# A planner's costs and ranks replaced: shorter VectorE and ScalarE costs, a weight-load lag ahead of products, and new ranks

## The chip, the cores and the metric

The kernel runs on one core of a Trainium2 chip. The metric is the device time in microseconds (us) of one execution. Engines are named as in the profile: PE is TensorE (PEld its weight loads), DVE is VectorE, ACT is ScalarE, POOL is GpSimd, and SP is SyncE, which here only issues DMAs.

## What is computed

A batch of 128 graphs with 128 nodes and 256 features goes through four layers. Each starts with a layer norm and a ReLU and adds its result to the residual x. Three layers are graph attention, one is a gated graph network of three GRU steps. Cut to what matters:

```python
def gat(h, adj, W, a):                      # layers 0, 1, 2
    Wh = einsum('bnf,fo->bno', h, W)
    e = (Wh @ a1)[:, :, None] + (Wh @ a2)[:, None, :]
    e = where(e > 0, e, 0.2 * e)
    att = softmax(where(adj > 0, e, -9e15), axis=-1)
    return elu(einsum('bij,bjo->bio', att, Wh))

def ggnn(x, adj, weight, w_ih, w_hh, b_ih, b_hh):   # layer 3
    A = (adj != 0)
    h = x
    for i in range(3):
        m = einsum('bnd,de->bne', h, weight[i])
        aggr = einsum('bst,bsd->btd', A, m)
        h = gru_cell(aggr, h, w_ih, w_hh, b_ih, b_hh)
    return h

for layer in (gat0, gat1, gat2, ggnn):
    x = x + layer(relu(layernorm(x)), adj)
```

All data is float32.

## The kernel before

**Groups and stages.** The 128 graphs are cut into 33 groups: one of two graphs, 31 of four, and one of two. Group g runs through three attention layers (`attention`, stages 0 to 2), a norm (stage 3, in `gat`), and three recurrent steps (`gru`, `step`). All groups share the engines; x has buffers for six groups in flight.

**An attention layer**, with the lines of the program before: VectorE's statistics (`stats`, L519), GpSimd's scaling and power for the inverse deviation (L525, L528), ScalarE's normalisation (xn, L602), VectorE's score sums (scr, L610, two for each graph). In the first two groups (`far` false) TensorE turns the scores into rows (L638) and the weights (L695), and VectorE scales them (at, L702). In later groups the rows go through DRAM (er), and the weights are transposed in blocks by VectorE (L552) and brought into place by two DMAs (d_at at L559, at at L563). Between lie ScalarE's slope (L649), VectorE's mask and maximum (L660, L662), ScalarE's exponential (L666) and scaling (L679). Then TensorE gathers neighbours (ahp, L723), ScalarE copies the sum (ah, L730), TensorE projects (hp, L742), and ScalarE and VectorE apply the ELU and add to x (L756, L758, L760).

**A recurrent step** is written as Strassen-like block products: TensorE aggregates in two halves (agp, L991), ScalarE copies each half (ag, L999), VectorE forms differences (t13, t24, L929, L923), TensorE makes the gate products (a, e, b, L965; nn, nnb, L952; ni, L1047), ScalarE and VectorE move partial sums between banks (L1015, L1099, L1106), ScalarE applies the tanh (L1035, L1052), VectorE mixes the new state. In the middle groups the new state is transposed by VectorE and sent through DRAM (`turned_state`, L580 and L584). The first two and the last two groups turn it on TensorE instead (hnp, L852).

**Setup.** Before the first recurrent step the weights are made: sums for the attention vectors (L325, L330), transposes of w_hh, w_ih and the layer weights (L410), products of w_ih with them (wcp, wcn, L466), ScalarE's copies out of the banks, and GpSimd's sums and differences of weight blocks (`combinations`, L388, L396).

**What sets the order.** No engine instruction is issued in the order of the program text. Every operation is handed to a planner (`Plan.add`) with its engine, an assumed cost in us, a rank, and the tiles that it reads and writes; a DMA (`Plan.load`) is an operation of SP with a cost of 0.45 and a landing time. `Plan.issue` then runs a list schedule: of the operations that are ready on an engine within `WINDOW` of the earliest, it takes the one of the lowest rank, and holds back those whose rank lies more than `AHEAD` (or, while the lowest rank left is up to `UNTIL`, `EARLY`) above the lowest rank still left. `lag` is what it adds between an operation and one that depends on it: per producing engine when another engine reads the result, nothing on the same engine. The list that comes out is issued as it stands; each engine then works through its own queue in that order on the chip, waiting on semaphores. The costs and ranks are thus used only to fix the order. They do not change what an instruction does.

Costs are given by the number of columns: `pe(c) = 0.006 + c/600`, `dve(c) = 0.145 + c/960`, `act(c) = 0.25 + c/1400`, `pool(c) = 0.35 + c/512`. Ranks come from tables: `SETUPS` for the setup, `ATT` for the stages of the first groups, `STARTS` for the recurrent steps of the first groups, and formulas (`stage`, `start`) for all later ones. Operations that empty a bank get the rank of their step less `URGENT`.

Of the kernel before, what the change touches and what calls it, by code (L numbers as in the profile page):

```python
# [14 lines left out]
P = 128  # L15
# [24 lines left out]
class Plan:  # L40
# [2 lines left out]

    LAG = {"PE": 0.26, "DVE": 0.2, "ACT": 0.2, "POOL": 0.15}
    WINDOW = 0.097
    AHEAD = 4.12
    EARLY = 5.00
    UNTIL = -1.46  # L50

    def __init__(self):
        self.ops, self.writers, self.readers, self.rings = [], {}, {}, {}
# [10 lines left out]
    def add(self, engine, cost, rank, fn, reads=(), writes=(), after=(), takes=()):  # L64


        reads = [k if isinstance(k, tuple) else (k, None) for k in reads]
        writes = [k if isinstance(k, tuple) else (k, None) for k in writes]
        vals = list(dict.fromkeys(v for v, _ in reads + writes))
        vals += [v for v in dict.fromkeys(takes) if v not in vals]  # L70
        op = Op(engine, cost, rank, fn, vals)
        for v in vals:
            v.ops.append(op)

        def others(book, key):
# [24 lines left out]
        for d in op.deps:  # L100
            d.users.append(op)
        self.ops.append(op)
        return op

    def lag(self, d, engine, data=True):
        if d.engine == "SP":
            return d.lands
        return 0.0 if d.engine == engine else self.LAG[d.engine] if data else 0.08

    def issue(self):  # L110
        waits_for = {op: len(op.deps) for op in self.ops}
# [77 lines left out]
def kernel(  # L189
# [25 lines left out]
    nc = tc.nc  # L215
# [25 lines left out]
    add, load = plan.add, plan.load  # L241
# [24 lines left out]
    def dve(cols):  # L266
        return 0.145 + cols / 960
# [12 lines left out]
    mhalf = const.tile([P, G], FT, name="mhalf")  # L280
    nc.vector.memset(mhalf, -0.5)

    SETUPS = [-4.77, -3.63, -3.63, -3.63, -3.63, -3.63, -3.63]
    setting = [0]

    def setup_rank():
# [18 lines left out]
    W, VA = [], []  # L305

    def attention_weights(l, w, a):
        rank = [-6.42, -7.21, -4.35][l]
        wt, va = const_val(f"w_{l}", [KD, D]), const_val(f"va_{l}", [2, D])
        first = [-11.17, -10.17, -7.80][l]  # L310
        load(256, first, lambda: nc.sync.dma_start(
            wt.t, w.rearrange("(k p) o -> p k o", p=P)), writes=[wt])
        ar = val(su, "ar", [2 * D], f"ar_{l}")
        load(2, first - 0.1, lambda: nc.sync.dma_start(
            ar.t[:1, :], a.rearrange("n o -> o n")), writes=[ar])

        ab = bank("gat", f"ab_{l}")
        add("PE", pe(T), rank, lambda: nc.tensor.matmul(
            ab.t, ones[:1, :], ar.t[:1, :], start=True, stop=True), reads=[ar], writes=[ab])
        wa = val(su, "wa", [2, KD], f"wa_{l}")  # L320
        vp = bank("gat", f"vp_{l}")

        def one(s, k):
            scr = val(su, "scr", [D], f"scr_{l}_{k}_{s}")
            add("DVE", dve(D) + 0.08, rank, lambda: nc.vector.scalar_tensor_tensor(  # L325
                scr.t, wt.t[:, k, :], 1.0, ab.t[:, s * D : (s + 1) * D], op0=OP.mult, op1=OP.mult,
                accum_out=wa.t[:, s, k : k + 1],
            ), reads=[wt, ab], writes=[scr, (wa, (s, k))])
            c = s * KD + k
            add("PE", 0.11, rank, lambda: nc.tensor.transpose(  # L330
                vp.t[:, c * P : (c + 1) * P], wa.t[:, s, k : k + 1].to_broadcast([P, P]), ident
            ), reads=[(wa, (s, k))], writes=[(vp, c)])

        for s in range(2):
            for k in range(KD):
                one(s, k)
        add("ACT", act(T), rank, lambda: nc.scalar.copy(
            va.t.rearrange("p s d -> p (s d)"), vp.t), reads=[vp], writes=[va])
        W.append(wt)
        VA.append(va)  # L340
# [195 lines left out]
                nm.t, st.t[:, :, 1], -1.0, None, op0=OP.mult), reads=[st], writes=[nm])  # L536
        return nm, rs

    def exchanged(srcs, cut, dst, name, n, rank):

        kd = len(srcs)
        f = kd * n * 32
        tr = val(gw, f"tr{kd}", [Q, kd * G * 32], f"tr_{name}", bufs=3 - kd)
        d = plan.val(
            dram, f"d{kd}_{n}", 2,
            lambda: dram.tile([Q, 32, Q, f], FT, tag=f"d{kd}_{n}", name=f"d_{name}"),
        )
# [20 lines left out]
    def turned_state(src, k, dst, name, n, rank):  # L570


        tr = val(gw, "trs", [G, P], f"tr_{name}", cut=n)
# [3 lines left out]
        add("DVE", dve(n * P), rank, lambda: nc.vector.transpose(  # L577
            tr.t.rearrange("p b j -> p (b j)"), src.t[:, k, : n * P]
        ), reads=[(src, k)], writes=[tr], takes=[d, dst])
        load(64 * n, rank, lambda: nc.sync.dma_start(d.t.rearrange("b p f -> p b f"), tr.t),  # L580
            reads=[tr], writes=[d])

        def back(j):
            load(16 * n, rank, lambda: nc.sync.dma_start(  # L584
                dst.t[j * 32 : (j + 1) * 32, : n * P].rearrange("c (m r) -> c m r", r=32),
                d.t[:, :, j * 32 : (j + 1) * 32].rearrange("b (q c) r -> c (b q) r", q=Q),
            ), reads=[d], writes=[(dst, j)])
# [240 lines left out]
    def gru(g, xt, am, hn0, h0):  # L828
# [39 lines left out]
        def flat(h):  # L868

            def part(k):  # L870
                add("DVE", 0.42, start(g, 0) - 1.0, lambda: nc.vector.tensor_copy(
                    cut(h.t[:, k, :TG]), first(k)), reads=[h0], writes=[(h, k)], after=[*after, *begun])

            for k in range(KD):
                part(k)

        def step(i, h):
# [202 lines left out]
            def mixed(c):  # L1080
# [50 lines left out]
        def end(h):  # L1131
# [40 lines left out]

    ATT = [
        [-8.90, -4.73, -3.23, -1.30],
        [-7.16, -4.64, -3.85, -2.65],
        [-3.70, -1.92, 1.59, 3.59],
        [-0.38, 1.67, 4.29, 4.81],
        [3.81, 5.72, 6.93, 8.03],
        [7.96, 10.27, 13.26, 12.41],
        [9.50, 11.75, 14.74, 15.00],  # L1180
        [12.46, 14.80, 17.00, 18.00],
        [15.66, 17.97, 20.00, 21.29],
        [18.50, 20.75, 23.00, 24.00],
    ]
    STARTS = [
        [1.68, 2.28, 4.42],
        [3.03, 4.63, 6.47],
        [5.97, 6.79, 10.50],
        [9.00, 11.18, 12.82],
        [12.28, 14.00, 16.00],  # L1190
        [14.67, 16.85, 19.17],
        [17.30, 19.87, 22.34],
        [21.00, 23.00, 25.06],
    ]
# [53 lines left out]
```

## Time and profile before

| | |
|---|---|
| median of three runs | 2569.77 us |
| lowest and highest run | 2566.48 and 2571.89 us |
| the profiled execution, its own time | 2566.74 us |
| its span, first to last instruction | 2565.0 us |
| DVE busy | 2105.9 us, 82% |
| ACT busy | 1768.5 us, 69% |
| POOL busy | 225.1 us, 9% |
| mean granted TensorE clock | 0.993 |

The page's list of engines is read as shares of the span; a busy TensorE means that some matmul is in flight, not that it works at its peak. The chain that ended last runs through TensorE for 95% of the span:

```profile
PE 95%; DVE 2%; ACT 2%; DMA 1%; issue 0%; SPq 0%; POOL 0%; ACTq 0%; DVEq 0%
```

The costliest groups of instructions show durations, which for VectorE and ScalarE are longer than the distance at which two of them can start one behind the other:

```profile
L610 DVE SCALAR_TENSOR_TENSOR scr<-xn,va 128x256 f32<-128x256 f32 x732 | 270.3, 418 | 36.1 <-ACT xn L602 35.8
L756 ACT ACTIVATE t<-hp 128x512 f32<-128x512 f32 x192 | 104.6, 595 | 201.3 <-PE hp L742 201.2
L758 DVE SCALAR_TENSOR_TENSOR x<-hp,x 128x512 f32<-128x512 f32 x192 | 124.0, 685 | 71.0 <-ACT t L756 70.9
```

After the bar stand the busy time in us, the mean duration in ns, and, after the second bar, the idle time of the engine ahead of these instructions with what ended it.

### The profile page before, as it was taken

The numbers are of one execution on the slowest core, as the hardware profiler recorded it, in microseconds if no ns is written. First come the engines' busy times: TensorE is split into PE (matmuls) and PEld (weight loads), VectorE is DVE, ScalarE is ACT, GpSimd is POOL, SyncE is SP. The second block draws the span as 40 slices with busy tenths as digits, with TensorE's granted clock in tenths as the row PEclk, the third lists the DMA queues.
The fourth block names the chain that finished last, engine by engine and source line by source line (L and its number), as shares of the span: only waits on it lengthen the run. The fifth ranks groups of instructions, "written<-read, shape, count | busy, mean of one in ns | idle before, by whom it ended". The sixth has DMA issues, their size and how long they took to land.

```text
span 2565.0 us, 39018 instructions
## 1 busy us (share of the span) xinstructions
PE 2527.7 (99%) x12549; PEld 2098.6 (82%) x12549; DVE 2105.9 (82%) x4955; ACT 1768.5 (69%) x4411; POOL 225.1 (9%) x328
## 2 busy tenths in 40 slices
PE   8799999999999999999999999999999999999998
PEld 5688888888888888888888888888888888888887
DVE  6778888888888888888888888888888888888765
ACT  6777676776766776766776666776666777666554
POOL 2210000000000000000000000000000000000000
PEclk8899999999999999999999999999999999999999
DMA  3113343343343333343334333333334443333320
GB/s 106 46 57 97 87 111 108 95 108 95 106 109 99 107 104 95 108 107 103 105 102 96 109 104 106 104 100 100 107 103 104 107 99 101 101 89 97 75 62 13
DMA packets 503123, 245.75 MB, mean 96 GB/s; under 512 B 280579, under 2 KB 472067, under 8 KB 502918
## 3 DMA queue, kind: packets, MB, share of 16 engines
q1 hardware_dynamic: 502918, 243.25, 35.3%
q8 instruction: 100, 1.64, 0.3%
q14 instruction: 105, 0.86, 0.1%
HBM read 139.28 MB, written 103.87 MB: 95 GB/s over the span
## 4 chain that ended last, share of the span: by engine, by line
PE 95%; DVE 2%; ACT 2%; DMA 1%; issue 0%; SPq 0%; POOL 0%; ACTq 0%; DVEq 0%
PE b L965 19%; PE hp L742 13%; PE e L965 13%; PE ni L1047 13%; PE a L965 13%; PE ahp L723 7%; PE agp L991 6%; PE nn L952 6%; PE nnb L952 5%; ACT em L666 0%; DVE scr L610 0%; ACT em L679 0%; PE hnp L852 0%; DMA at<-d_at 0%; ACT hn L791 0%
## 5 line engine op out<-in xcount | busy, mean ns | idle before, releaser
L742 PE MATMUL hp<-w,ah 128*128 128x256 f32 x1536 | 356.2, 384 | 0.5 <-ACT ah L730 0.5
L1047 PE MATMUL ni<-ag,wc_n 128*128 128x512 f32 (+1 forms) x792 | 352.9, 580 | 0.9 <-DVE ni L1041 0.9
L742 PEld LDWEIGHTS hp<-w,ah 128*128 128x128 f32 x1536 | 286.7, 191 | 61.9 <-ACT ah L730 13.1
L610 DVE SCALAR_TENSOR_TENSOR scr<-xn,va 128x256 f32<-128x256 f32 x732 | 270.3, 418 | 36.1 <-ACT xn L602 35.8
L1047 PEld LDWEIGHTS ni<-ag,wc_n 128*128 128x128 f32 x792 | 147.1, 190 | 125.2 <-issue 104.0
L756 ACT ACTIVATE t<-hp 128x512 f32<-128x512 f32 x192 | 104.6, 595 | 201.3 <-PE hp L742 201.2
L1052 ACT ACTIVATE wn<-ni,bi 128x512 f32<-128x512 f32 (+1 forms) x198 | 133.4, 674 | 157.5 <-PE ni L1047 114.5
L991 PEld LDWEIGHTS agp<-am,hn 128*128 128x128 f32 x1536 | 204.7, 191 | 42.7 <-issue 30.8
L991 PE MATMUL agp<-am,hn 128*128 128x128 f32 x1536 | 208.9, 275 | 3.6 <-ACT ag L999 3.0
L525 POOL TENSOR_SCALAR ve<-st 128x4 f32<-128x4 f32 (+1 forms) x132 | 28.4, 215 | 2087.8 <-DVE st L519 1735.5
L965 PE MATMUL a<-h,whh_rz 128*128 128x256 f32 (+1 forms) x792 | 208.8, 373 | 0.8 <-ACT z L1035 0.5
L723 PEld LDWEIGHTS ahp<-at,xn 128*128 128x128 f32 x1536 | 190.6, 196 | 23.0 <-issue 14.4
L602 ACT ACTIVATE xn<-x,nm,rs 128x256 f32<-128x256 f32 x366 | 201.1, 594 | 3.8 <-DVE nm L531 3.8
L965 PE MATMUL a<-ag,wc_rz 128*128 128x256 f32 (+1 forms) x792 | 199.1, 373 | 0.0
L723 PE MATMUL ahp<-at,xn 128*128 128x128 f32 x1536 | 192.5, 279 | 4.6 <-DMA at<-d_at 2.8
L758 DVE SCALAR_TENSOR_TENSOR x<-hp,x 128x512 f32<-128x512 f32 x192 | 124.0, 685 | 71.0 <-ACT t L756 70.9
L519 DVE BATCH_NORM_STATS2 st<-x 128x6 f32<-128x512 f32 x256 | 170.3, 690 | 2.6 <-DMA x<-in_x_dram 2.5
L649 ACT ACTIVATE em<-er,e 128x128 f32<-128x128 f32 x366 | 164.3, 523 | 2.4 <-DMA er<-de 2.3
L666 ACT ACTIVATE em<-em,nmx 128x128 f32<-128x128 f32 x384 | 149.4, 392 | 11.6 <-DVE nmx L662 11.4
L965 PEld LDWEIGHTS a<-h,whh_rz 128*128 128x128 f32 x792 | 140.9, 191 | 16.9 <-issue 0.7
L965 PEld LDWEIGHTS a<-ag,wc_rz 128*128 128x128 f32 x792 | 141.1, 191 | 15.2 <-issue 0.5
L528 POOL TENSOR_TENSOR rs<-ve,mhalf 128x4 f32<-128x4 f32 (+1 forms) x132 | 144.0, 1091 | 11.0
(158 smaller groups left out, 5541.3 us busy)
## 6 DMA issues: line engine op xcount, KB each, us to landing
d_hn<-tr_hn SPq DMA_DIRECT2D x116, 256.0 KB, 2.4
hn<-d_hn SPq DMA_DIRECT2D x464, 64.0 KB, 2.3
er<-de SPq DMA_DIRECT2D x90, 256.0 KB, 3.9
d_at<-tr_at SPq DMA_DIRECT2D x90, 256.0 KB, 2.2
at<-d_at SPq DMA_DIRECT2D x360, 64.0 KB, 2.0
x<-in_x_dram SPq DMA_DIRECT2D x31, 512.0 KB, 5.0
d_h<-tr_h SPq DMA_DIRECT2D x31, 512.0 KB, 2.7
h<-d_h SPq DMA_DIRECT2D x124, 128.0 KB, 2.7
```

What stands on the lines that cost most here:

```text
L519: add("DVE", dve(T), rank, lambda: nc.vector.bn_stats(st.t[:, b, :].rearrange("p b s -> p (b s)"), xt.t[:, b, :].rearrange("p b d -> p d b ...
L528: add("POOL", 1.04, rank, lambda: nc.gpsimd.tensor_tensor(rs.t, ve.t, mhalf[:, :n], op=OP.pow), reads=[ve], writes=[rs])
L602: add("ACT", 0.45, rank, lambda: nc.scalar.activation(xn.t[:, b, :], xt.t[:, b, :], AF.Relu, bias=nm.t[:, b : b + 1], scale=rs.t[:, b : b ...
L610: add("DVE", dve(D), rank, lambda: nc.vector.scalar_tensor_tensor(scr.t, xn.t[:, b, :], 1.0 if far else rs.t[:, b : b + 1], VA[l].t[:, s, ...
L649: add("ACT", 0.55 if far else 0.42, rank, lambda: nc.scalar.activation(em.t[:, b, :], e2_row(b), AF.Prelu, bias=e.t[:, 0, b : b + 1], alph ...
L666: add("ACT", 0.42, rank, lambda: nc.scalar.activation(em.t[:, b, :], em.t[:, b, :], AF.Exp, bias=nmx.t[:, b : b + 1], accum_out=sm.t[:, b ...
L723: add("PE", pe(P), rank, lambda: nc.tensor.matmul(summed(ps, b), xn.t[:, b, k * P : (k + 1) * P], turned_weights(b), start=True, stop=True ...
L742: add("PE", pe(D), rank, lambda: nc.tensor.matmul(hp.t[:, b * D : (b + 1) * D], ah.t[:, k, c * P : (c + 1) * P], W[l].t[:, k, :], start=(k ...
L952: op = add("PE", pe(H), at, lambda: nc.tensor.matmul(ps.t[:, o : o + H], WHH[1].t[:, blk, :], rhs(), start=starts, stop=True, skip_group_c ...
L965: nc.tensor.matmul(ps.t[:, gate * D : gate * D + H], w[0].t[:, blk, gate * P : (gate + 1) * P], rhs(), start=go, stop=w is not WHH, skip_g ...
L991: nc.tensor.matmul(ps.t[:, b * P : (b + 1) * P], s, am.t[:, b, :], start=True, stop=True)
L1047: add("PE", pe(TG), rank + 0.45 + 0.05 * c, lambda k=k: nc.tensor.matmul(ni[c].t[:, :TG], WC[i][1].t[:, k, c * P : (c + 1) * P], ag.t[:, k ...
```

## The change

The planner's assumptions and the ranks are replaced; no operation is added, removed or altered.

- **Costs.** VectorE operations over 0.3 us are planned 0.08 shorter (but at least 0.08), the others 0.02 shorter; ScalarE operations 0.10 shorter.
- **Lags.** A result of VectorE, ScalarE or GpSimd for another engine is planned 0.02, 0.04 and 0.05 later. A result that the same engine reads is now planned 0.10 (VectorE, ScalarE) or 0.05 (GpSimd) later, where it was 0. Whatever TensorE needs of an engine other than itself and SP gets 0.25 more (`TO_PE`), also where it only waits for a bank or buffer to come free.
- **Ranks.** New numbers in `SETUPS`, in the attention weights' ranks, in `ATT` (15 groups given by hand instead of 10) and `STARTS`, a new formula for later groups (`LATE`), new `AHEAD`, `EARLY`, `UNTIL` and `URGENT`.
- **Separate ranks.** In `exchanged` the VectorE transposes take a rank of their own (`later`), used for the final output; in `turned_state` the DMAs take `rank - 1.0` of the step, and the transpose keeps `quick`.

```diff
-    LAG = {"PE": 0.26, "DVE": 0.2, "ACT": 0.2, "POOL": 0.15}
-    WINDOW = 0.097
-    AHEAD = 4.12
-    EARLY = 5.00
-    UNTIL = -1.46
+    LAG = {"PE": 0.26, "DVE": 0.22, "ACT": 0.24, "POOL": 0.2}
+    SELF = {"DVE": 0.1, "ACT": 0.1, "POOL": 0.05}
+    TO_PE = 0.25
+    WINDOW = 0.09700
+    AHEAD = 3.80719
+    EARLY = 4.99516
+    UNTIL = 4.33848
...
+        if engine == "DVE":
+            cost = max(0.08, cost - 0.08) if cost > 0.3 else cost - 0.02
+        elif engine == "ACT":
+            cost -= 0.1
         op = Op(engine, cost, rank, fn, vals)
...
-        return 0.0 if d.engine == engine else self.LAG[d.engine] if data else 0.08
+        if d.engine == engine:
+            return self.SELF.get(engine, 0.0) if data else 0.0
+        return (self.LAG[d.engine] if data else 0.08) + (self.TO_PE if engine == "PE" else 0.0)
...
-    SETUPS = [-4.77, -3.63, -3.63, -3.63, -3.63, -3.63, -3.63]
+    SETUPS = [-6.84787, -3.92921, -3.63418, -3.63418, -3.49802, -3.63418, -4.69368]
...
-        rank = [-6.42, -7.21, -4.35][l]
+        rank = [-7.18052, -6.81219, -4.64144][l]
...
-        first = [-11.17, -10.17, -7.80][l]
+        first = [-11.17390, -10.51150, -3.60698][l]
...
-    def exchanged(srcs, cut, dst, name, n, rank):
+    def exchanged(srcs, cut, dst, name, n, rank, later=0.0):
...
-            add("DVE", dve(n * P), rank, lambda: nc.vector.transpose(
+            add("DVE", dve(n * P), rank + later, lambda: nc.vector.transpose(
...
-        load(64 * n, rank, lambda: nc.sync.dma_start(d.t.rearrange("b p f -> p b f"), tr.t),
+        load(64 * n, moved, lambda: nc.sync.dma_start(d.t.rearrange("b p f -> p b f"), tr.t),
...
-                    turned_state(hnew, c, ahead[c], f"hn_{g}_{i + 1}_{c}", n_g, quick)
+                    turned_state(hnew, c, ahead[c], f"hn_{g}_{i + 1}_{c}", n_g, quick, rank - 1.0)
...
-                    o, f"o_{g}", n_g, rank,
+                    o, f"o_{g}", n_g, rank, 1.0 - URGENT,
...
-    URGENT = 1.00
-    SPAN = 2.25
-    HEAD = 5.5
+    URGENT = 0.99051
...
-    LEAD = 8.5
+    LATE = [-7.38300, -5.94660, -3.05880, -2.41780]
...
-        [-8.90, -4.73, -3.23, -1.30],
-        [-7.16, -4.64, -3.85, -2.65],
-        [-3.70, -1.92, 1.59, 3.59],
+        [-10.03150, -5.73666, -4.29186, -3.57801],
+        [-6.37019, -5.24915, -3.99721, -2.27005],
+        [-3.69791, -1.82237, 1.40914, 4.51073],
...
-        [1.68, 2.28, 4.42],
-        [3.03, 4.63, 6.47],
+        [1.67988, 2.28262, 3.67109],
+        [2.73703, 4.08406, 6.35165],
...
-        return ATT[g][l] if g < len(ATT) else 3.0 * g - LEAD + (SPAN * l if l < 3 else HEAD)
+        return ATT[g][l] if g < len(ATT) else 3.0 * g + LATE[l]
...
-        return STARTS[g][i] if g < len(STARTS) else 3.0 * g + 2.0 * i
+        return STARTS[g][i] if g < len(STARTS) else 3.0 * g + [0.0, 2.00000, 4.00000][i]
```

More of the change, by code (lines that the diff above doesn't have):

```diff
@@ L568, in exchanged, with turned_state @@
             back(j)
-    def turned_state(src, k, dst, name, n, rank):
+    def turned_state(src, k, dst, name, n, rank, moved):
         tr = val(gw, "trs", [G, P], f"tr_{name}", cut=n)
@@ L579, in turned_state @@
         ), reads=[(src, k)], writes=[tr], takes=[d, dst])
-        load(64 * n, rank, lambda: nc.sync.dma_start(d.t.rearrange("b p f -> p b f"), tr.t),
+        load(64 * n, moved, lambda: nc.sync.dma_start(d.t.rearrange("b p f -> p b f"), tr.t),
             reads=[tr], writes=[d])
         def back(j):
-            load(16 * n, rank, lambda: nc.sync.dma_start(
+            load(16 * n, moved, lambda: nc.sync.dma_start(
                 dst.t[j * 32 : (j + 1) * 32, : n * P].rearrange("c (m r) -> c m r", r=32),
@@ L870, in part @@
             def part(k):
-                add("DVE", 0.42, start(g, 0) - 1.0, lambda: nc.vector.tensor_copy(
+                add("DVE", 0.42, start(g, 0) - URGENT, lambda: nc.vector.tensor_copy(
                     cut(h.t[:, k, :TG]), first(k)), reads=[h0], writes=[(h, k)], after=[*after, *begun])
@@ L1170 @@
     NNR = 0.25
-    LEAD = 8.5
+    LATE = [-7.38300, -5.94660, -3.05880, -2.41780]
     ATT = [
-        [-8.90, -4.73, -3.23, -1.30],
-        [-7.16, -4.64, -3.85, -2.65],
-        [-3.70, -1.92, 1.59, 3.59],
[L1177 to L1183, printed above, removed]
+        [-10.03150, -5.73666, -4.29186, -3.57801],
+        [-6.37019, -5.24915, -3.99721, -2.27005],
+        [-3.69791, -1.82237, 1.40914, 4.51073],
+        [-1.21335, 2.94736, 3.53217, 4.28927],
+        [3.27576, 4.87639, 7.15969, 9.03665],
+        [8.55092, 10.98350, 13.51910, 13.24740],
+        [10.20170, 12.51510, 13.94510, 15.66230],
+        [13.68410, 16.44050, 18.86210, 20.30620],
+        [15.59690, 17.95450, 18.50160, 23.00030],
+        [18.45420, 20.96390, 22.85330, 24.29900],
+        [22.61700, 24.05340, 26.94120, 27.58220],
+        [25.61700, 27.05340, 29.94120, 30.58220],
+        [28.61700, 30.05340, 32.94120, 33.58220],
+        [31.61700, 33.05340, 35.94120, 36.58220],
+        [34.61700, 36.05340, 38.94120, 39.58220],
     ]
     STARTS = [
-        [1.68, 2.28, 4.42],
-        [3.03, 4.63, 6.47],
[L1188 to L1193, printed above, removed]
+        [1.67988, 2.28262, 3.67109],
+        [2.73703, 4.08406, 6.35165],
+        [5.98936, 8.53152, 10.05390],
+        [9.67922, 12.11970, 12.62760],
+        [12.27650, 13.52560, 16.00000],
+        [15.60350, 16.50370, 19.23710],
+        [17.36150, 20.71520, 22.17790],
+        [21.77790, 23.54310, 24.41420],
     ]
     def stage(g, l):
-        return ATT[g][l] if g < len(ATT) else 3.0 * g - LEAD + (SPAN * l if l < 3 else HEAD)
+        return ATT[g][l] if g < len(ATT) else 3.0 * g + LATE[l]
     def start(g, i):
-        return STARTS[g][i] if g < len(STARTS) else 3.0 * g + 2.0 * i
+        return STARTS[g][i] if g < len(STARTS) else 3.0 * g + [0.0, 2.00000, 4.00000][i]
     work, h = {}, {}
```

## The prediction

> **What bounds the kernel now.** I read the page first, then busy time by stage, then TensorE's waits, then the timeline of the worst stretch. From the page:
>
> ```profile
> span 2565.0 us, 39018 instructions
> ...
> PE 2527.7 (99%) x12549; PEld 2098.6 (82%) x12549; DVE 2105.9 (82%) x4955; ACT 1768.5 (69%) x4411; POOL 225.1 (9%) x328
> ...
> PEclk8899999999999999999999999999999999999999
> ```
>
> TensorE is the bound. By stage (start:end, length, then busy time of PE, its weight loads, DVE, ACT and POOL with their instructions, the granted clock, DMA share and GB/s):
>
> ```profile
> 0.00:25.00 25.00, 19.23 (x65) 12.34 (x65) 15.16 (x58) 12.42 (x36) 3.10 (x10) 0.73 0.70 208
> 25.00:50.00 25.00, 21.37 (x102) 15.85 (x103) 19.15 (x62) 18.72 (x55) 9.22 (x16) 0.93 0.17 53
> 50.00:75.00 25.00, 20.35 (x83) 13.15 (x82) 17.73 (x54) 17.99 (x52) 14.43 (x19) 0.96 0.10 22
> 75.00:100.00 25.00, 18.41 (x84) 15.08 (x84) 16.92 (x45) 17.99 (x52) 3.94 (x7) 0.77 0.11 33
> 100.00:150.00 50.00, 44.48 (x298) 39.99 (x297) 38.69 (x109) 36.34 (x106) 5.61 (x7) 1.00 0.24 69
> 150.00:200.00 50.00, 48.76 (x281) 42.33 (x280) 40.70 (x113) 40.32 (x107) 5.37 (x7) 1.00 0.19 59
> 200.00:500.00 300.00, 297.52 (x1464) 246.62 (x1463) 246.94 (x578) 212.28 (x523) 24.44 (x34) 1.00 0.38 100
> 500.00:2300.00 1800.00, 1800.00 (x8852) 1500.09 (x8852) 1531.90 (x3560) 1263.98 (x3124) 147.85 (x211) 1.00 0.39 103
> 2300.00:2500.00 200.00, 199.58 (x953) 163.06 (x953) 145.19 (x307) 117.56 (x280) 11.17 (x18) 1.00 0.29 76
> 2500.00:2565.00 65.00, 58.05 (x379) 50.14 (x377) 33.47 (x77) 30.86 (x83) 0.00 (x0) 0.97 0.04 13
> ```
>
> The reader is to see three stages. From 500 to 2300 us there is no idle time at full clock: an order can win nothing there, only lose. In the first 100 us TensorE idles 20.6 us (5.8 + 3.6 + 4.7 + 6.6) and the clock is short. From 100 to 500 it idles 9.2 us (5.5 + 1.2 + 2.5), and from 2300 on 7.4 us. All idle together is 37.3 us.
>
> As a check, both programs have 6349 matmuls: 1903 of 128 columns, 4059 of 256, 387 of 512. Back to back at full clock they start 0.222, 0.433 and 0.86 us apart in the timeline (two records each). The sum, 422 + 1758 + 333 = 2513 us, lies 52 us under the span; the 15 us that are not idle time belong to the half clock. **52 us, 2%, is all that there is to win.** Below, "work" at a matmul is this full-clock sum over all matmuls ahead of it in TensorE's order; time minus work is what has been lost by then.
>
> The waits are small and have many causes:
>
> ```profile
> PE atp L695 <- ACT ah L730: 3.4, 1, 3.4
> PE agp L991 <- ACT ag L999: 3.0, 2, 2.3
> PE ahp L723 <- DMA at<-d_at: 2.8, 2, 2.0
> ```
>
> (total us, times, longest.)
>
> **The change part by part.** It adds and removes no instruction: each engine issues the same operations in another order, DMAs included. So every cost is a wait that comes or goes.
>
> *The planner's costs.* The issue distance, not the duration, is what the queue pays: 512-wide VectorE operations take 0.69 us but start 0.60 apart, 512-wide ScalarE ones take 0.60 and start 0.49 apart. The old plan used 0.68 and 0.62, the new one 0.60 and 0.52, with 0.10 for a result that the same engine reads. The new costs are thus near the trace, not too short. The 0.25 us added ahead of a product is near the 0.19 us of one weight load.
>
> *Steady part, 500 to 2300 us.* Cost 0. I compared, per kind of round trip (product, other engine, next product), the TensorE work placed between. The shortest ones grow: projection behind its copy L730 from 0.87 to 1.10 us, b behind its copy L1099 from 0.87 to 1.30, b behind VectorE's sum L1106 from 1.30 to 2.16. One place grows more frequent: the second half of aggregation (L991) stands 1.30 us behind the first, whose copy L999 it needs, in 47 of 72 steps instead of 23. The copy takes 0.57 us and at those 23 places TensorE never idled, so I take 0.
>
> *Stretch from 100 to 500 us.* With measured durations and without queueing, 12 round trips here were too short for their work, by 3.7 us in all; in the new order 4 are, by 0.8. I take 3.3 us off the 9.2 (ends: 7 off, or 2 more, since queues on ScalarE made the longest wait, 2.3 us at L991).
>
> *The first 100 us.* These end with the first recurrent product at 100.95 us; work before it is 68.5 us in both orders, so 32.4 us is lost. The chain of group 1 (four graphs, three attention layers) sets it. I follow it with durations of the trace.
> 1. x of group 1 is now loaded after w_1. 256 KB at the first window's 208 GB/s make it 1.2 us later; VectorE covers that with layer 1's four setup sums (L325). The eight score sums (L610), before from 14.8 to 19.7 us, should end near 17: 2.5 us gained.
> 2. It is lost again: 3.8 us of setup transposes (whh, w_ih, gt_0) now stand between the turned weights L695 and the product L723 that uses them, and each waits for ScalarE to empty a bank. I put L723 of group 1 at 29.5 us, against 28.7. But 2.4 us more work is done there. In the loads, w_hh goes ahead of adj_3, whose issue blocked the queue for 6.1 us; this keeps those transposes supplied.
> 3. Layer 1: L695 of group 1 starts at 51.9 us; I expect 52, but with 40.1 us of work behind it instead of 35.4.
> 4. Layer 2: two weight products (1.7 us) no longer stand in the chain ahead of L723 and L742, four transposes (0.9) do: 0.8 us. GpSimd's power (L528) no longer queues behind weight sums: 0.9 us. Scores collide with five weight sums instead of seven: 0.9 us (below). Together 2.6: L695 starts near 78.4 us, against 80.97.
> 5. The products of group 2 (L723) waited 2.0 us for their weights from DRAM. Their transpose (L552) now follows group 1's L702 directly, not two residual sums, their wait and a statistic (4 us): the wait goes. The transposes L806 move ahead of L723 and no longer wait 0.8.
>
> Sum: 2.6 + 2.0 + 0.8 = **5.4 us**. What is late next is ScalarE's copy L999 of the first step, as now. Ends: 0, if steps 2 and 3 eat it, and 14, if the chain also keeps the 2.5 us of step 1 and the clock stays up (half of 11.5 us, below).
>
> *Two places where rules of the Trainium skill bear on this.* The row first:
>
> ```profile
> 68.94 0.93 DVE L610 SCALAR_TENSOR_TENSOR scr<-xn,rs,va 128x256 f32<-128x256 f32 x1
> ...
> 72.07 0.47 DVE L610 SCALAR_TENSOR_TENSOR scr<-xn,rs,va 128x256 f32<-128x256 f32 x1
> ```
>
> While GpSimd adds weight blocks (L388), a score sum takes 0.93 us, not 0.47. The Trainium skill, "SBUF — State Buffer", section "Who interferes with whom", says that a VectorE operation with two SBUF inputs and a reading GpSimd one exclude each other, and the second waits for the whole of the first. In the new order wc_1's five sums stand right behind the power L528, beside these same scores. By the row that costs 5 x 0.46 = 2.3 us on the chain, by the rule 5 x 0.72 (one sum alone) = 3.6; against the seven of the old order the gain is 0.9 by the row, 1.4 by the rule. I take the row.
>
> Second, in the new order the four transposes L695 of group 1's layer 2 follow its score rows L638 with nothing between, though two softmax passes, the exponentials and the scaling lie there: between 5 and 6 us of idle TensorE in one piece (from L660 at 75.16 to L695 at 80.97 the old order took 5.8, but filled some of it; its longest idle piece was 3.4). The skill's "TensorE: Matmul & The Clock Gate", section "Why this matters for your kernels", warns of gaps over about 3 us: the clock halves. The row 75 to 100 us already shows 0.77, 11.5 us at half clock, so by the row nothing is added; by the rule, which asks for at least 4 us of busy time to return, some 2 us. I take 0.
>
> *Tail, after 2300 us.* The last eight groups of matmuls stand alike in both orders; 0, ends 1 either way.
>
> *DMAs.* In SP's queue, where a DMA that waits holds up all behind it, DMAs of the steady part move by up to 32 places, some two thirds of a group's. From the product that feeds them to the one that needs them at least 16.0 us of work lie for the states (L580, L584; 13.0 before) and 19.1 for the attention weights (L559, L563; 21.2 before). Two legs take 2.4 + 2.3 us in the list of DMAs, so the work still hides them: 0. If the cover were gone, a wait like the 2.0 us above would come once per layer and group.
>
> **The sum.** 5.4 + 3.3 + 0 + 0 = 8.7 us off. The profiled execution took 2566.74 us (span 2565.0 and 1.7 around it), so 2558.0; the median of the three runs, 2569.77, lies 3.0 higher, so **2561.0 us**.
>
> **The rivals.**
> - *Much more* (2549, on the median's scale as all here): the fill reaches its upper end, 14, and 100 to 500 gives 7: 2569.8 - 21. For it: lost time in the fill is 32 us, and new costs fit. Against: the chain's own operations don't shrink. Chance 0.13.
> - *No change* (2567): the chain of group 1 stays where it is, step 5 is replaced by another late result, and only the 3 us after 100 remain. For it: in step 2 the gain is lost once already. Chance 0.17.
> - *Slower* (2575): the 1.30 us behind copy L999. At 0.57 us for the copy plus drain and weight load, about 0.26 us is to spare; one 0.49 us ScalarE operation ahead of the copy makes a wait of 0.23 to 0.3 us. In 47 steps, scaled from 72 to all 93, that is 61 waits and up to 18 us; with 8.7 gained elsewhere 2579, with every third step hit 2567, so it decides once about half are hit: 2575 at three quarters (46 x 0.3 = 14). Against: 23 of them show no wait now. Chance 0.12.
> - *Forecast* 0.58.
>
> **How the numbers follow.** About 0.2%, 5.1 us, is what runs of this kernel can tell: faster means under 2564.6. That is the forecast (0.58) and the first rival (0.13): 0.71. Within: 0.17; slower: 0.12. The range, 2549 to 2571, holds the first rival's time, the forecast and "no change"; it leaves out most of the slower case and a little below.
>
> **What would show it.** Busy TensorE of 1800 in the 1800 us after 500; idle time in the first 100 us near 15; L695 of group 1's layer 2 after one idle piece of over 4 us; no wait for at<-d_at near 95 us; the first L991 near 95 us. Wrong if waits for L999 appear in the steady part, or if the first L991 stays at 101.

## The result, and the profile after

The changed kernel takes **2583.64 us** (median of 4 runs, 2583.12 to 2584.46), the kernel before 2568.12 (4 runs, 2566.37 to 2571.89, three of them the runs of the table above): a ratio of 1.0059 with an interval of 1.0041 to 1.0076. It is 15.5 us slower where 8.7 us less were predicted, and outside the predicted range.

From the page of the changed kernel, span, busy time and TensorE clock:

```profile
span 2581.7 us, 39074 instructions
...
PE 2533.1 (98%) x12549; PEld 2098.1 (81%) x12549; DVE 2046.1 (79%) x4955; ACT 1746.7 (68%) x4411; POOL 220.2 (9%) x328
...
PEclk9899999999999999999999999999999999999999
```

The same stages as before (start:end, length, busy PE, PEld, DVE, ACT, POOL, clock, DMA share, GB/s):

```profile
0.00:25.00 25.00, 19.16 (x55) 12.14 (x55) 13.59 (x57) 13.08 (x38) 3.13 (x10) 1.00 0.70 208
25.00:50.00 25.00, 23.20 (x122) 16.62 (x122) 19.05 (x56) 18.63 (x52) 11.66 (x18) 1.00 0.19 53
50.00:75.00 25.00, 19.16 (x89) 12.92 (x87) 20.07 (x63) 19.28 (x56) 13.09 (x18) 1.00 0.10 22
75.00:100.00 25.00, 15.92 (x71) 13.21 (x72) 15.94 (x45) 17.01 (x49) 3.95 (x7) 0.73 0.11 33
...
200.00:500.00 300.00, 298.59 (x1470) 246.57 (x1469) 245.44 (x593) 208.70 (x516) 27.53 (x36) 1.00 0.37 102
500.00:2300.00 1800.00, 1789.12 (x8763) 1486.22 (x8762) 1467.47 (x3520) 1237.98 (x3110) 139.58 (x211) 1.00 0.38 102
```

The reader is to see the row of 500 to 2300 us: TensorE, which had no idle time there, idles 10.9 us, at full clock. The first 100 us idle 22.6 us (5.8 + 1.8 + 5.8 + 9.1) instead of 20.6; 15 were predicted.

The clock of 1.00 in the first row isn't a measured full clock. The clock records of this profile begin at 24.4 us, and a stretch without records is printed as 1.00. Up to 23 us TensorE's records (two for each product) start 0.22 us (128 columns) and 0.43 us (256) apart, twice the distances that they keep later: the first 24 us ran at half clock, as they mostly did before.

Idle time is only part of what a wait costs: at the place of 1168 us below, TensorE is idle for 0.28 us, but the next product starts 0.44 us later than back to back. So I measure **lost time**: the start-to-start distance of TensorE's instructions less what they take back to back (0.111 us for 128 columns, 0.2165 for 256, 0.432 for 512), summed by stage. Half clock counts in it too. A product leaves two records in the trace, each of these lengths; a transpose leaves one.

| lost time, us | 0–50 | 50–100 | 100–200 | 200–500 | 500–2300 | from 2300 | sum |
|---|---|---|---|---|---|---|---|
| before | 21.6 | 19.4 | 10.3 | 4.1 | -0.6 | 7.1 | 61.9 |
| after | 18.3 | 22.0 | 9.8 | 3.0 | 18.8 | 6.6 | 78.5 |

The sums differ by 16.6 us, as the spans do (16.7). The whole loss, 19.4 us, lies in the steady part; the gain elsewhere is 2.8.

TensorE's waits of the changed kernel in the steady part, 500 to 2300 us (total, times, longest; lines of the changed program lie 8 higher in this region, so L999 is the former L991 and L1007 the former L999):

```profile
PE agp L999 <- ACT ag L1007: 5.8, 21, 0.3
PE ni L1055 <- ACT ag L1007: 2.7, 12, 0.2
PE ni L1055 <- DVE ni L1049: 1.6, 7, 0.2
```

Two small waits, each about once in a group's 78 us. The timeline of the changed kernel around one of the first kind (start, duration, engine, line):

```profile
1165.47 1.05 PE L999 MATMUL agp<-am,hn 128*128 128x128 f32 x8
...
1165.83 0.60 ACT L799 ACTIVATE hn<-x,nm,rs 128x256 f32<-128x256 f32 x1
...
1166.32 0.54 ACT L657 ACTIVATE em<-er,e 128x128 f32<-128x128 f32 x1
...
1166.74 0.48 ACT L1043 ACTIVATE r<-b,brz 128x256 f32<-128x256 f32 x1
...
1167.10 0.48 ACT L1043 ACTIVATE z<-b,brz 128x256 f32<-128x256 f32 x1
...
1167.46 0.59 ACT L1007 COPY ag<-agp 128x512 f32<-128x512 f32 x1
...
1168.10 0.71 PE L999 MATMUL agp<-am,hn 128*128 128x128 f32 x4 [0.28 <-ACT ag L1007]
```

The first half of aggregation has ended by 1166.5, but its copy starts at 1167.46, 1.99 us after the products: ScalarE still has a normalisation, a slope, r and z ahead of it, back to back. The second half, 1.3 us of work behind the first, waits. In the kernel before, the places with the same 1.3 us of work look like this; the copy starts 0.79 us after the last of its products, and nothing waits:

```profile
1215.99 0.61 PE L991 MATMUL agp<-am,hn 128*128 128x128 f32 x4
1216.19 0.69 ACT L1052 ACTIVATE wn<-ni,bi 128x512 f32<-128x512 f32 x1 [0.98 <-PE ni L1047]
...
1216.78 0.57 ACT L999 COPY ag<-agp 128x512 f32<-128x512 f32 x1
...
1217.73 1.05 PE L991 MATMUL agp<-am,hn 128*128 128x128 f32 x8
```

At the second kind of place two normalisations stand ahead of r, which VectorE's `ni` needs, and of the copy; the profile names the copy for 12 of these waits and VectorE for 7:

```profile
1217.45 1.10 ACT L610 ACTIVATE xn<-x,nm,rs 128x256 f32<-128x256 f32 x2
...
1218.43 0.47 ACT L1043 ACTIVATE r<-b,brz 128x256 f32<-128x256 f32 x1
...
1218.88 1.29 DVE L1049 SCALAR_TENSOR_TENSOR ni<-r,wn 128x512 f32<-128x512 f32 x2
...
1219.72 2.81 PE L1055 MATMUL ni<-ag,wc_n 128*128 128x512 f32 x6 [0.22 <-ACT ag L1007]
```

Two normalisations take 1.10 us with 0.60 each, so they start 0.49 to 0.50 apart (median in the steady part, from an xn to whatever follows it at once, 273 pairs: 0.492). r and z start 0.36 apart. The new plan counts 0.45 - 0.10 = **0.35 us** for a normalisation and 0.363 for r and z. It takes the dearer one for the cheaper.

### The profile page after: what moved, and what is told of

The parts are those of the page before. It is cut to its first block, busy times and chain, and to the rows that moved or that the text cites. A ratio compares the mean times of both kernels' runs of the same rounds, so it can differ in the third digit from the quotient of the medians.

```text
span 2581.7 us, 39074 instructions
## 1 busy us (share of the span) xinstructions
PE 2533.1 (98%) x12549; PEld 2098.1 (81%) x12549; DVE 2046.1 (79%) x4955; ACT 1746.7 (68%) x4411; POOL 220.2 (9%) x328
## 4 chain that ended last, share of the span: by engine, by line
PE 75%; ACT 17%; DVE 5%; issue 1%; POOL 1%; DMA 0%; SPq 0%; POOLq 0%; DVEq 0%; ACTq 0%
PE b L973 13%; PE ni L1055 12%; PE hp L750 12%; PE a L973 11%; PE e L973 8%; PE ahp L731 6%; PE agp L999 5%; PE nn L960 5%; ACT xn L610 3%; PE nnb L960 2%; ACT z L1043 2%; ACT r L1043 2%; ACT em L687 2%; ACT hn L799 2%; ACT wn L1016 2%; ACT em L674 2%
## 5 line engine op out<-in xcount | busy, mean ns | idle before, releaser
L999 PEld LDWEIGHTS agp<-am,hn 128*128 128x128 f32 x1536 | 210.8, 191 | 46.6 <-ACT ag L1007 19.0
L999 PE MATMUL agp<-am,hn 128*128 128x128 f32 x1536 | 222.0, 277 | 8.6 <-ACT ag L1007 8.5
L973 PE MATMUL a<-h,whh_rz 128*128 128x256 f32 (+1 forms) x792 | 201.6, 373 | 0.0
L657 ACT ACTIVATE em<-er,e 128x128 f32<-128x128 f32 x366 | 176.1, 532 | 3.7 <-DMA er<-de 3.7
L738 ACT COPY ah<-ahp 128x512 f32<-128x512 f32 (+1 forms) x198 | 113.0, 573 | 65.2 <-PE ahp L731 64.5
L674 ACT ACTIVATE em<-em,nmx 128x128 f32<-128x128 f32 x384 | 150.2, 396 | 8.0 <-DVE nmx L670 4.6
```

Source lines behind the costliest of these rows:

```text
L657: add("ACT", 0.55 if far else 0.42, rank, lambda: nc.scalar.activation(em.t[:, b, :], e2_row(b), AF.Prelu, bias=e.t[:, 0, b : b + 1], alph ...
L674: add("ACT", 0.42, rank, lambda: nc.scalar.activation(em.t[:, b, :], em.t[:, b, :], AF.Exp, bias=nmx.t[:, b : b + 1], accum_out=sm.t[:, b ...
L973: nc.tensor.matmul(ps.t[:, gate * D : gate * D + H], w[0].t[:, blk, gate * P : (gate + 1) * P], rhs(), start=go, stop=w is not WHH, skip_g ...
L999: nc.tensor.matmul(ps.t[:, b * P : (b + 1) * P], s, am.t[:, b, :], start=True, stop=True)
```

## The experiments

At first two suspects stood: planned costs that are too short (theory A) and the new ranks of the late groups (B); C, D, Q and F came with later runs. "Before" was run beside each at 2567.35 to 2568.96 us.

**1. The changed kernel with the old ScalarE costs.**

```diff
-        elif engine == "ACT":
-            cost -= 0.1
```

> The changed kernel with ScalarE's costs as they were before (the 0.1 is not taken off); VectorE's costs, lags and ranks stay new. Theory A (the plan now thinks ScalarE faster than it is, so that operations without haste stand ahead of a copy or a sigmoid that TensorE waits for): the waits in the steady part go, idle TensorE from 500 to 2300 us falls from 10.9 us to under 2, and the time falls to 2563 to 2569. Theory B (the new ranks of the late groups bring the waits, whatever the costs): idle time there stays at 8 or more and the time at 2580 to 2587.

Measured 2596.27 us (2593.21 to 2597.19), ratio 1.0105 (1.0088 to 1.0122). Lost time from 100 to 500 us rose from 12.8 to 29.0, and the steady part lost 14.1, now in other waits (for d_at, b and c). A forecast of theory A that failed. All of ScalarE's costs together are no clean trial of one of them, since every order in the entry changes too; but it also says that a cost of 0.45 for the normalisations, near the measured 0.49, isn't enough by itself for a steady part without loss.

**2. The changed kernel with the old formula for late groups.**

```diff
-        return ATT[g][l] if g < len(ATT) else 3.0 * g + LATE[l]
+        return ATT[g][l] if g < len(ATT) else 3.0 * g - 8.5 + (2.25 * l if l < 3 else 5.5)
```

> The changed kernel with the old formula for the ranks of the attention stages from group 15 on; costs, lags and all else stay new. Theory B (ranks): the waits go in the steady part that these ranks order, and the time falls to 2563 to 2570. Theory A (ScalarE's costs): waits of 0.2 us or more for a ScalarE copy or a VectorE seed come again, at these or other places, idle time from 500 to 2300 us stays at 6 or more, and the time stays above 2577.

2581.08 us (2579.74 to 2581.85), ratio 1.0044 (1.0029 to 1.0059). The steady part still loses 16.8 us, and the time is what theory A forecast. But the sum hides where. The formula acts from group 15 on, and TensorE's order is that of the changed kernel up to 1019 us. Lost time in us, cut finer:

| lost time, us | 500–1000 | 1000–1400 | 1400–2300 |
|---|---|---|---|
| before | 0.0 | -0.1 | -0.5 |
| changed kernel | 5.2 | 4.1 | 9.5 |
| kernel 2, old late formula | 5.5 | 8.3 | 2.9 |
| kernel 4, new costs and lags on old ranks | 11.8 | 1.1 | 2.8 |
| kernel 5, cost of xn and hn put right | 1.5 | 0.3 | 0.2 |

After a costly passage from one formula to the other, the waits that return in every group are gone, with the short costs still in place. From the changed kernel and from kernel 2:

```profile
1400.00:2300.00 900.00, 894.25 (x4378) 742.52 (x4377) 731.89 (x1752) 616.43 (x1550) 68.56 (x106) 1.00 0.38 102
```

```profile
1400.00:2300.00 900.00, 899.69 (x4412) 749.85 (x4411) 748.00 (x1782) 623.15 (x1567) 67.72 (x105) 1.00 0.38 102
```

The wait behind a normalisation, a slope, r and z comes 21 times in the changed kernel and 4 times here, all before 933 us. So B isn't refuted: the new late ranks are part of the cause.

**3. The changed kernel with xn and hn 0.14 us dearer** (0.49 after the subtraction, the measured distance).

```diff
-            add("ACT", 0.45, rank, lambda: nc.scalar.activation(
+            add("ACT", 0.59, rank, lambda: nc.scalar.activation(
```

> The changed kernel with one cost alone put right: the normalisations xn and hn are planned at 0.49 us, the distance at which they start in the trace, instead of 0.35. Theory A in its narrow form (these 16 operations of a group are what is planned too short): the waits behind xn and hn in ScalarE's queue go, idle time from 500 to 2300 us falls to 0 to 4 us, time 2563 to 2572. Theory B: no change, 2580 to 2587.

2579.37 us (2578.89 to 2579.79), ratio 1.0038 (1.0023 to 1.0053). The steady loss falls from 18.8 to 3.4, and idle time there to 1.9 us, as the narrow form of A forecast; the time is outside its forecast. From 50 to 500 us 46.5 us are lost instead of 34.8: the same number also reorders the fill (TensorE's order differs from 31 us on). So cause and side effect had to be parted.

**4. The kernel before with the new costs and lags, old ranks.**

```diff
+    SELF = {"DVE": 0.1, "ACT": 0.1, "POOL": 0.05}
+    TO_PE = 0.25
...
+            cost = max(0.08, cost - 0.08) if cost > 0.3 else cost - 0.02
...
+            cost -= 0.1
```

> The kernel before with the new costs and lags alone; all ranks, AHEAD, EARLY and UNTIL stay old. Theory A: the short ScalarE costs bring waits to the steady part here too, over 5 us of idle TensorE from 500 to 2300 us (it was 0), and the time is 2575 or more. Theory B: the steady part stays without idle time, and the time lies within 6 us of before.

2605.88 us (2604.65 to 2606.88), ratio 1.0141 (1.0126 to 1.0156). Steady loss 15.7; the first recurrent product comes at 114.3 us. Theory A's forecast came true in time and idle time (6.1 us), but hardly for its reason: 10.4 of the 15.7 us are lost before 800 us, the longest waits are for b and d_at, and the second half of aggregation waits for its copy only once.

**5. As 3, but from the tenth group on.** `0.59 if g >= 10 else 0.45`, for xn and hn. ScalarE's order stays that of the changed kernel up to 607 us, TensorE's up to 676 us.

> The changed kernel, with the planned cost of the normalisations xn and hn raised by 0.14 us (to the measured 0.49) for groups from the tenth on only; the order of the first 300 us or so stays as it is in the changed kernel. Theory A (the steady loss comes from this one cost being too short): the lost time from 500 to 2300 us falls from 18.8 to under 4 us, from 200 to 500 it stays near 3, the waits behind the copy ag and behind ni are gone, and the time is 2566 to 2570 us. Theory B (the steady loss comes from the new ranks or lags, and the cost only moved it elsewhere): at least 2578 us, with other waits once per group.

2566.00 us (13 runs, 2564.38 to 2568.53), ratio 0.9994 (0.9986 to 1.0002). The steady row and the place that answers to 1165 to 1168 us above:

```profile
500.00:2300.00 1800.00, 1799.10 (x8842) 1498.52 (x8842) 1481.83 (x3562) 1242.28 (x3132) 139.63 (x211) 1.00 0.38 103
```

```profile
1158.83 1.10 ACT L799 ACTIVATE hn<-x,nm,rs 128x256 f32<-128x256 f32 x2
1158.97 1.05 PE L999 MATMUL agp<-am,hn 128*128 128x128 f32 x8
1159.82 0.48 ACT L1043 ACTIVATE r<-b,brz 128x256 f32<-128x256 f32 x1
...
1160.17 0.48 ACT L1043 ACTIVATE z<-b,brz 128x256 f32<-128x256 f32 x1
1160.53 0.59 ACT L1007 COPY ag<-agp 128x512 f32<-128x512 f32 x1
...
1161.17 0.71 PE L999 MATMUL agp<-am,hn 128*128 128x128 f32 x4
```

The slope now stands behind the copy, which starts 1.56 us after the products instead of 1.99, and the second half has no wait. Lost time is 2.0 us in the steady part (18.8) and 3.0 from 200 to 500, as in the changed kernel. One number, in two lines, takes 16.8 us of loss out of the steady part; the median, 15.5 us above the kernel before, comes to 1.4 us below it. **A is shown in the narrow form: the planned cost of the two normalisations brings the loss, on these ranks.** With kernel 2 it makes a pair: the loss that returns in every group needs both the short cost and the new late ranks, and putting either right removes most of it. No run raised another cost by as much, so it isn't shown that only this number would do; but kernel 3, with another order from 31 us on, comes down to 3.4 us as well.

**6. The new ranks with the old costs and lags.**

> The new ranks with the old costs and lags; with the earlier run of the new costs on the old ranks (2606 us) it fills the table of two by two. Theory C (ranks fit only the lags they were made with): in the planned order the second half of aggregation now follows the first with no work between in 14 of 72 steps, where it has to wait for the copy, some 1.2 us each, 17 us in the steady part, and the fill isn't better than before: 2590 to 2610 us. Theory D (the ranks are good by themselves and only the costs do harm): 2560 to 2568 us.

2778.98 us (2777.05 to 2782.71), ratio 1.0824 (1.0809 to 1.0839), far beyond what either theory gave. TensorE's waits of this kernel:

```profile
PE a L965 <- DVE h L871: 81.8, 23, 6.7
PE agp L991 <- ACT ag L999: 20.9, 22, 2.8
PE b L965 <- DVE e L1106: 18.5, 18, 4.2
```

The forecast 17 us behind the copy are the second line; the first, a new group's state copied too late for its first gate product, wasn't foreseen. D falls; C holds in direction. The table of two by two, in us:

| | old ranks | new ranks |
|---|---|---|
| old costs and lags | 2567–2569 | 2779 |
| new costs and lags | 2606 | 2584 |

Neither half of the change can be priced alone.

**7. The changed kernel with de of group 3 kept behind at of group 2** by a rule in the plan (a DMA dependency).

```diff
+                after=backs["at_2_0"] if (g, l) == (3, 0) else ())
```

> The changed kernel, with the DMA that stores the scores of group 3's first layer (de) kept behind the four DMAs that fetch group 2's weights (at) in the DMA queue; nothing else of the plan's rules is touched. Theory Q (the products of group 2 at 93 us wait because their fetch stands in the queue behind de, which waits for scores until 88.3 us): the fetch is issued at about 87.2 instead of 88.7 us, the wait at 93 us falls from 2.7 to about 1.2 us and the first recurrent product comes at about 99 instead of 100.3 us; the time is 2581 to 2584 us, since the steady part keeps its loss. Rival: the weights are late by themselves (transpose and first leg), the fetch is issued at 88.7 again, and the wait stays at 2.7 us.

2599.18 us (2595.95 to 2600.04), ratio 1.0120 (1.0106 to 1.0133). The wait is gone and the first recurrent product comes at 96.4 us, but the plan answered one constraint with another order everywhere: 24.5 us lost in the steady part and as much from 100 to 500 us (12.8 in the changed kernel). As a test of the wait it says yes; as a test of the time it says nothing.

**8. The kernel before with xn and hn planned 0.10 shorter** from the tenth group on.

> The kernel before, with the planned cost of xn and hn cut by 0.10 us (to the 0.35 that the change plans) from the tenth group on, all else old. Theory A1 (a normalisation planned too short makes steady waits in any plan): 5 to 18 us lost from 500 to 2300 us, 2573 to 2587 us. Theory A2 (it does so only where it stands with r and z ahead of a copy on which a product 1.30 us later depends; here the 23 places with 1.30 us keep the ELU's exponential and two tanh ahead of the copy, as before): 0 to 3 us, 2567 to 2572 us.

2569.26 us (2567.35 to 2571.96), ratio 1.0006 (0.9998 to 1.0014), steady loss 0.6. A2 holds: by itself the short cost does no harm in the old order. At its 23 places with 1.3 us of work between the halves one tanh stands right ahead of the copy, which starts 0.8 to 0.9 us after its products.

**9. As 5, with one DMA moved in the finished list:** de of group 3 behind the four fetches at of group 2. No other queue changes.

> The changed kernel with the right cost of xn and hn from the tenth group on, and, when the plan is finished, one DMA moved in SP's queue: the store of group 3's scores (de) behind the four fetches of group 2's weights (at). No other instruction changes its place on any queue, which the earlier try by a rule in the plan didn't achieve. Theory Q: the fetch is issued 1 to 1.5 us earlier (87.2 instead of 88.5), the wait of the products of group 2 at 93 us falls from 1.9 us (2.7 in the changed kernel) to under 1 us; the time is 1 us below that kernel without the move, 2564 to 2566. Rival: the weights are late by their transpose and first leg alone, and the wait is unchanged.

In the changed kernel (SPq is the DMA queue):

```profile
84.83 0.32 SPq L567 DMA_DIRECT2D d_at<-tr_at  x1
...
88.30 0.32 SPq L637 DMA_DIRECT2D de<-e  x1
...
88.73 1.79 SPq L571 DMA_DIRECT2D at<-d_at  x4
...
93.07 1.20 PE L731 MATMUL ahp<-at,xn 128*128 128x128 f32 x4 [2.69 <-DMA at<-d_at]
```

In kernel 9, whose lines lie 16 higher:

```profile
83.64 0.32 SPq L583 DMA_DIRECT2D d_at<-tr_at  x1
...
85.71 1.76 SPq L587 DMA_DIRECT2D at<-d_at  x4
87.57 0.38 SPq L653 DMA_DIRECT2D de<-e  x1
...
90.05 2.05 PE L747 MATMUL ahp<-at,xn 128*128 128x128 f32 x16 [0.98 <-DVE x L782]
```

The fetch follows the store d_at after 2.1 us instead of 3.9: it had stood in the queue behind de, whose scores weren't ready. The wait for weights is gone (1.85 us in kernel 5, whose orders are otherwise the same); what is left, 0.98 us, is put down to VectorE's residual sum. Q is shown. The median, 2565.59 us (2563.60 to 2568.17), is as forecast, but its 0.4 below kernel 5 is no more than the runs scatter.

**10. As 9, with three more moves on group 1's chain.**

```diff
+        ("de_3_0", "at_2_0", 1),
+        ("st_0_3", "nmx_1_2", 1),
+        ("power_2_0", "share_1_2", 4),
+        ("sums", "half_0", 5),
```

Each line: what is moved, behind what, how many at most.

> As the last, with three more moves in the finished plan, all on the chain of group 1's layer 2: the five weight sums of GpSimd go behind its scaling of x of group 0 (they overlapped the score sums and made them 0.9 us long), the first statistic of group 0's norm goes behind group 1's row maximum on VectorE (0.6 us in the chain), and two exponentials of group 2 go behind group 1's scaling on ScalarE (0.8 us in the chain). Theory F (these, not the number of setup products, hold the transposes of group 1 at 80 us): they start at about 76.8 instead of 79.7 us, the idle piece ahead of them is 3.5 instead of 6.4 us, and the time is 2561 to 2564. Rival: TensorE waits the same time elsewhere, behind group 2's weights or group 3's scores that the moved sums now slow down: 2565 to 2568.

2563.55 us (11 runs, 2561.77 to 2565.92), ratio **0.9983** (0.9975 to 0.9992): below both kernels. A score sum beside GpSimd's weight sums, and the transposes, in the changed kernel:

```profile
70.53 0.99 DVE L618 SCALAR_TENSOR_TENSOR scr<-xn,rs,va 128x256 f32<-128x256 f32 x1
...
80.32 1.35 PE L703 MATMUL atp<-ident,em 128*128 128x128 f32 x4 [6.44 <-ACT em L687]
```

and in kernel 10 (19 lines higher):

```profile
69.10 0.48 DVE L637 SCALAR_TENSOR_TENSOR scr<-xn,rs,va 128x256 f32<-128x256 f32 x1
...
76.97 1.36 PE L722 MATMUL atp<-ident,em 128*128 128x128 f32 x4 [5.49 <-ACT em L706]
```

The transposes start near the forecast 76.8, but part of that is scatter between profiles: kernel 9 already stands 1.2 us ahead of the changed kernel there, in an order that is the same. From group 1's first score row (L646, L662 and L665) to its transposes it takes 10.0 us in the changed kernel and in kernels 5 and 9, and 8.1 in kernel 10. The moves are thus worth 1.9 us where 2.9 were forecast, and the median is 2.0 below kernel 9's. The idle piece shrinks by 1.0 us only, since the score rows ahead of it end sooner as well. F holds for the place and for two thirds of the gain. The next wait for hn grew by 0.8 us, and the copy `ag` of the first recurrent step, near 100 us, costs 2.6 and 2.7 us in kernels 9 and 10.

## Why the prediction was wrong

- **The steady part, "Cost 0", failed** at the sentence "The new costs are thus near the trace, not too short". I had compared only 512-wide operations. For VectorE the check holds at 256 columns too (planned 0.332, distance 0.345), and for ScalarE at r and z. For the normalisations it doesn't: planned 0.35, distance 0.49, and the old 0.45 had been the better number. The second sentence that failed is "at those 23 places TensorE never idled, so I take 0": it looked at TensorE's work between the halves and not at ScalarE's work ahead of the copy. Together with the new late ranks this cost 19.4 us of the 25.4 by which the forecast missed the profiled span (16.7 more where 8.7 less were predicted). The exponentials (L674), too, are planned short, 0.32 against 0.39 with the reading of their sum; kernel 5 shows that the steady part doesn't need them put right.
- **A rule that I passed over gives the number.** The Trainium skill, "ScalarE: Activation LUTs", section "What ACT_TABLE_LOAD costs", gives an activation 186 ns plus 0.833 ns per column, 93 more for each of bias and scale that is a column of values per partition, and 93 less back to back. For xn and hn, which have both, this makes an estimate of 186 + 213 + 186 - 93 = 492 ns; the trace shows 492. The 512-wide copy has neither, which is why it couldn't stand for them. One flat subtraction of 0.10 for all ScalarE operations can't be right for both.
- **The rival "Slower" was the right mechanism:** the second half of aggregation, 1.30 us behind its first half, waits when ScalarE has more work ahead of the copy. I gave it 0.12 because 23 such places had shown no wait, and hadn't looked at what stands ahead of the copy there. In the trace of the changed kernel there are two kinds: at 22 places, with two exponentials ahead, the copy starts 0.7 us after its products, and nothing waits, as at the 23 of before; at 21 it starts 2.0 us after them, and every one waits. The rival was also too small for one wait, 0.3 us: 0.44 us is lost at each, and a second place (ni), which it didn't name, waits nearly as often and loses 9.4 us against 11.4 here.
- **A sum that was wrong: "52 us is all that there is to win".** It took two records for each of the 6349 matmuls. The 149 transposes among them leave one, 0.11 us from the next, and the plan counts 0.11 for them too. The work is thus 16.5 us less in all, 9.9 less ahead of the first recurrent product, and the loss of before is 61.9 us in the table above. The forecast doesn't rest on the sum, but steps 2 and 4 count transposes at twice their length (3.8 us for 17 of them, 0.9 for four).
- **Steps 1 to 3 of the first 100 us:** score sums end at 18.3 us (predicted 17; before they ended at 19.4, not at 19.7 as I had read); the products of group 1's layer 0 start at 30.8 (29.5 predicted); its layer 1 transposes at 54.4 (52 predicted). So the chain is 2.4 us later there than I allowed; that the added setup work is the reason is likely, not shown. By 50 us the loss is 3.3 us smaller, by 100 it is only 0.6.
- **Step 4:** 80.3 us, predicted 78.4. The start was already late, and what I left out were operations of other groups inside the chain: a statistic between mask and maximum (0.6 us) and two exponentials ahead of the scaling (0.8). GpSimd's five sums did make scores 0.99 and 0.93 us long, as the row of before had it, but only these two, one of 0.60 and a residual sum of 1.20 (0.69 in kernel 10): 1.6 us in all, where the row made 2.3 for five scores and the rule 3.6. Experiment 10 moved all three, and the chain became 1.9 us shorter.
- **Step 5 failed:** the wait for d_at near 93 us didn't go, it is 2.7 us. The transpose was early enough; the fetch wasn't, behind de in SP's queue. The prediction weighed that queue for the steady part only. Experiment 9 shows it.
- **100 to 500 us:** 1.6 us gained of the 3.3; right in sign. **Tail:** 0.6 gained where 0 was taken.
- **Clock:** the idle piece of over 4 us came as foretold (6.4), and half clock around it. By the clock records it lasts 13.7 us between 70 and 100 us in both kernels, in one piece before and in two after: taking 0 was right.

What stays open: which of the new late ranks lets the short cost do its harm; which of the new lags and costs besides xn and hn matter for the fill, and for the steady loss of kernels 1 and 4; and why the new ranks need the new lags so badly. Kernel 6 shows where its time goes, not which lag would save it.

## What to carry to other kernels

A planner's cost error is dangerous not by its size alone but by what stands next to it: with the normalisations planned 0.14 us too short, a slope found room ahead of a copy with nothing to spare, once in every group, and together with the second place this cost 17 to 19 us. In an order with something to spare a cost 0.14 us short did nothing (experiment 8). Check each planned cost against the start-to-start distance of that very form, by operands as well as by width, before any ranks are fitted to it. And after a plan is fitted, move single instructions in the finished list rather than change its rules, if an effect is to be measured or a last few us won: a new cost or rule reorders everything behind it (experiments 3 and 7), a move does what it says (9 and 10: no other instruction of any queue changed its place). And a sum over a long stage can hide that a remedy works in part of it: cut it finer before a theory is dropped (experiment 2).

## What the runs showed of the hardware

- A granted clock of 1.00 in a row can mean that there are no clock records: in the changed kernel and in kernel 5 they begin at 24.4 and 23.1 us, and until then TensorE's records start at twice their later distance. The distances tell. Kernel 9, with TensorE's order the same there, has 3.4 us of full clock from 5.9 us on and gained nothing by it: by 50 us kernels 5 and 9 had lost 17.7 and 18.1 us.
- Kernel 5 and the changed kernel issue the same orders up to 607 us, yet their first recurrent product came at 98.5 and 100.3 us. A difference of 2 us in the fill between two profiles isn't an effect.
- VectorE and GpSimd hold each other up. Beside GpSimd's weight sums two score sums take 0.99 and 0.93 us instead of 0.48, and each ends 0.28 us after the GpSimd sum beside it; a score at 73.86 us, where one of GpSimd's sums ends and the next starts, takes 0.47. GpSimd's five operations take 4.50 us in all there and 4.15 in kernel 10, where they run apart from group 1's scores.
